# Four transformer layers on one core: capacity search and sorts with buffers of their own, norms on ScalarE, a float32r gate and up product, single PSUM banks, and score steps that give way

## The chip, the cores and the metric

The kernel runs on one core of a Trainium2 chip. The metric is the device time of one execution in microseconds (us). A time is the median of several runs. Besides these there is one execution under the hardware profiler. Its trace gives all durations used here.

The engines of the core are named as the profile names them: PE (TensorE, with PEld for its weight loads), DVE (VectorE), ACT (ScalarE), POOL (GpSimd) and SP (SyncE, which here only issues DMA transfers).

## What is computed

The input is 16 sequences of 256 tokens with 128 features, so 4096 rows. Four layers follow one another. Each adds an attention-like branch and a feed-forward branch to the residual stream, both computed from the same layer norm:

```python
xn = _layernorm(x)
x = x + _L0_attn_ref(xn, ...) + _L0_ffn_ref(xn, ...)
xn = _layernorm(x)
x = x + _L1_attn_ref(xn, ...) + _L1_ffn_ref(xn, ...)
xn = _layernorm(x)
x = x + _L2_attn_ref(xn, ...) + _L2_ffn_ref(xn, ...)
xn = _layernorm(x)
x = x + _L3_attn_ref(xn, ...) + _L3_ffn_ref(xn, ...)
```

- Layer 0: 16-head attention with rotary positions. The feed-forward part has 8 experts of width 512; each token chooses two, and each expert keeps only the `cap` tokens with the highest gates:

```python
cap = max(math.ceil(t * TOP_K * CAP_FACTOR / N_EXPERTS), 1)
for e in range(N_EXPERTS):
    g_masked = jnp.where(has, gate, -jnp.inf)
    vals, idx = jax.lax.top_k(g_masked, cap)
    h = jax.nn.relu(xe @ W1[e]) @ W2[e]
    y = y.at[idx].add(g[:, None] * h)
```

- Layer 1: a linear recurrence along the sequence, a shared expert, and 15 experts of width 128 of which each token takes three.
- Layer 2: attention again, and 8 experts of width 512 of which each token takes one.
- Layer 3: causal attention with a linear position bias per head, an output projection, and a dense gated unit with integer weights:

```python
gate = jnp.einsum('bsd,hd->bsh', x, wg)   # wg = w_gate / 127
up = jnp.einsum('bsd,hd->bsh', x, wu)
h = jax.nn.silu(gate) * up
return jnp.einsum('bsh,dh->bsd', h, wd)
```

## The kernel before

**Tiles.** The rows are cut into 8 blocks of 512 (`BLK`), held in SBUF for the whole kernel (`xb`). A block is two sequences. Expert layers sort their tokens by expert in groups of blocks: two groups of four blocks in layers 0 and 2, four groups of two in layer 1 (`GRP`). Sorted tokens lie in DRAM tables; an expert's tile is 128 rows of such a table.

**Who sets the order.** Nothing is issued while the layers are described. Each engine call goes through `Engine.__getattr__` (L318) into `Plan.add`, which gives it an estimated cost. `Plan.order` (L186) then runs a list schedule over all operations, with a key per operation made of a wanted time per stage (`WANTED`) less the length of the longest chain behind it. It also hands out buffers: a tile has a tag, a tag has a ring of slots, and `room` (L227) says whether a slot is to be had. In the pools `work` and `small` the tiles of a tag are given out in turn, task by task, within one stream (`Plan.run` names the stream). The resulting order is fixed on each engine, and the engines wait for one another through semaphores. Almost every instruction of the profile therefore has one line, L350 (the recorded call); groups are told apart by tile names.

**Attention.** For each sequence `front` (L895) makes the scores once to get row maxima, and `back` (L941) makes them again transposed, with the maxima subtracted, for the exponentials. Head size is 8, so a head's product uses 32 of the 128 rows of the PE array, a strip; heads go two strips at a time. A sequence has 8 score steps in `front` and 8 in `back`; with 16 sequences and three attention layers these are 768 steps. In layers 0 and 2 a `front` step is 4 matmuls of 256 columns and a `back` step 4 of 256 and 2 of 512. In layer 3 each step has 8 strip matmuls and 2 whole-array ones in bfloat16 that hide later keys. When the scheduler takes a step, it looks for another one ready at that moment that uses the other two strips, and weaves the two (`woven`, L74): a pair. Otherwise the step is issued alone.

**PSUM.** There are eight banks. `front` puts its two score tiles into one tile of two banks (`two_banks`, L436), of which there is one in all. One DVE `tensor_reduce` takes the maxima of both banks (in layer 3 two, for the two halves of the queries). The other six banks are single ones (`one_bank`, L439) that everything else shares.

**Norms.** `normalize` (L552) takes mean and variance on DVE (`moments`) and then applies them on DVE, with one `tensor_scalar` for each 128 rows: 4 for each block and layer, 128 in all.

**Capacity search and sorts.** `route_0` (L1090) makes the gates of layer 0 into `g0`. `capacity` (L627) then finds each expert's threshold bit by bit in 30 rounds; a round is a compare and a reduce on DVE, a small matmul `tot_b` that adds over partitions, and three small DVE steps. Its two large tiles `cap_cmp` and `cap_above`, and the tile `m` of `sort` (L1214), share the tag `cap` with three slots; search and sorts run in the same stream, `"sort"`. `ranks` (L673) uses one slot with tag `rank` for both. `sort` gives each token its row in the sorted table; `scatter` (L719) writes the rows there with indirect DMAs on POOL. Only when a group's rows are written can `some_tiles` (L1274) fetch the tiles (`xs`) and run its experts: transpose (`trs`), first product (`ph`), second product (`po`), result back to DRAM. `combine` (L775) gathers results (`yg`) and adds them with the gates, which need the search's result.

**Layer 3's dense unit.** `weights_3` (L1312) loads the integer weights and scales them to float32. `ffn_3` (L1325) runs, for each block and each of three slices of 128 hidden units, two matmuls of 128x512 in float32 (`pp`), a tanh on ACT, two DVE steps, and afterwards the down product.

Of the kernel before, what the change touches and what calls it, by code (L numbers as in the profile page):

```python
# [24 lines left out]
P = 128  # L25
# [8 lines left out]
GRP = {0: 4, 1: 2, 2: 4, 3: 2}  # L34
COLD = 1.2
# [3 lines left out]
    "": (62.9, 0.0, 0.0, 0.0),  # L39
    "att0": (-17.7, 39.8, 36.9, 120.1),  # L40
    "att2": (-125.2, 4.9, -67.1, 45.9),
    "att3": (-85.1, 46.0, 51.1, 102.8),
    "bias2": (-56.2, 153.4, 126.8, 401.9),
    "f3": (166.9, 61.0, 85.4, -51.3),
    "ffn0": (-34.4, 0.0, 32.5, 0.0),
    "ffn1": (2.9, 54.3, 149.0, 145.3),
    "ffn2": (-212.1, 0.0, -158.9, 0.0),
    "kept": (-12.8, 0.0, 0.0, 0.0),
    "rec": (31.1, 105.4, 174.5, 249.2),
    "route0": (-57.1, 0.0, -13.2, 0.0),  # L50
    "route1": (-194.8, -8.3, -27.9, 172.0),
    "route2": (-57.3, 0.0, 43.4, 0.0),
    "sort0": (238.4, 0.0, 310.5, 0.0),
    "sort1": (-45.0, 52.9, 68.6, 170.5),
    "sort2": (-13.5, 0.0, -51.0, 0.0),
    "sum0": (-25.8, 151.2, -71.0, 129.0),
    "sum1": (99.1, 130.3, 136.1, 252.2),
    "sum2": (51.9, 205.8, 84.3, 182.0),
}
EPS = 1e-5  # L60
# [26 lines left out]
class Plan:  # L87
# [98 lines left out]
    def order(self):  # L186
# [40 lines left out]
        def room(o):  # L227

            new = [self.ring_of[x] + (x,) for x in o.tiles if x not in placed]
            for g, turn, task, _, x in new:  # L230
                mine = [y for h, _, _, _, y in new if h is g]
                held = task is not None and (x not in turn[: len(mine)] if task["begun"] else bool(turn))
                if held or len(g["free"]) < len(mine):
                    return g, 0.0, new
            at = [sorted(g["free"])[sum(h is g for h, *_ in new) - 1][0] for g, *_ in new]
            return None, max(at, default=0.0), new
# [18 lines left out]
        while True:  # L255
# [17 lines left out]
            take(o, new, t)  # L273
            cost, pair = o.cost, None
            if o.strips:
                for item in sorted(now[e]):
                    p = item[1]
                    if p.strips and not any(x in o.strips for x in p.strips):
                        short, at, new = room(p)
                        if short is None and at <= t:  # L280
                            now[e].remove(item)
                            heapq.heapify(now[e])
                            take(p, new, t)
                            both = [(x.cost - x.rest, x.rest) for x in (o, p)]
                            cost, pair = max(x for x, _ in both) + max(sum(x for _, x in both) - 0.24 * COLD, 0.0), p
                            break
            if e == "PE" and quartered != bool(o.strips):
                cost, quartered = cost + 0.15 * COLD, bool(o.strips)
# [23 lines left out]
class Engine:  # L312
# [5 lines left out]
    def __getattr__(self, method):  # L318
        real = getattr(self.real, method)

        def call(*args, **kw):
# [8 lines left out]
            if self.name == "PE":  # L330
# [6 lines left out]
                else:  # L337
                    cost = max(size(args[2]), T) / 4800
                    strip = args[1].offset // args[1].ap[0][0]
# [12 lines left out]
        return call  # L352

# [57 lines left out]
def four_layers(ctx: ExitStack, tc: tile.TileContext, a: dict, out: bass.AP, at: dict, found=None):  # L411
# [24 lines left out]
    def two_banks(name):  # L436
        return ps.tile([P, 2, BLK], F32, tag="s", bufs=1, name=name)

    def one_bank(name):  # L439
        return ps.tile([P, BLK], F32, tag="o", bufs=6, name=name)  # L440
# [111 lines left out]
    def normalize(srcs, dst_of, name):  # L552

        mv, rs = moments(srcs, name)
        for i, src in enumerate(srcs):
            dst = dst_of(i)
            for t in range(BT):
                k = i * BT + t
                V.tensor_scalar(
                    dst[:, t, :], src[:, t, :], mv[:, k, 0:1], rs[:, k : k + 1], ALU.subtract, ALU.mult  # L560
                )
# [65 lines left out]
    def capacity(g):  # L627
# [37 lines left out]
        run, _ = ranks(cmp, E0, NT, "cap")  # L665
# [7 lines left out]
    def ranks(m, ne, n, name):  # L673
# [839 lines left out]
```

## Time and profile before

| what | value |
|---|---|
| runs (5): median, lowest, highest | 1570.53, 1549.61, 1579.18 us |
| profiled execution: device time | 1544.55 us |
| its span, first to last instruction | 1542.8 us |
| outside the span | 1.75 us |
| mean granted PE clock | 0.921 |
| DMA moved | 267.35 MB, 173 GB/s over the span |

The page of the profile gives each engine's busy time, then the span in 40 equal slices (38.6 us each) with busy tenths, granted clock and DMA share; then the chain of work that ended last; then the costliest groups of instructions, with their mean duration and the idle time before them. A busy PE in these records is not a PE at its peak: matmuls overlap and a matmul at half clock is busy for longer. Further answers of the trace used here are: windows (busy time of each engine in chosen stretches, with clock and DMA share), one tile's instructions with first and last start, the instructions in order of time, who waited for whom, and groups kept apart by shape.

### The profile page before, as it was taken

To read this page: it belongs to the slowest core of one execution; us is meant where nothing else is said; L and a number is where in the kernel's file an instruction comes from. 1 tells how busy PE (TensorE), PEld (TensorE's weight loads), DVE (VectorE), ACT (ScalarE), POOL (GpSimd) and SP (SyncE) were. 2 spreads that over 40 slices of the span, in tenths; PEclk is the share of its full clock that TensorE was granted. 3 is DMA by queue.
4 is the path that set the end of the run, shared out by engine and by line. 5 is a ranking of instruction groups with operands and counts; after the bars stand their busy time and mean duration, and the time that the engine had idled before them with its cause. 6 is when DMAs were issued, how large, how long until landed. Compare 5 with 4: busy or idle time off the path is not lost. (4 is left out here: it accounts for less than half of the span.)

```text
span 1542.8 us, 35056 instructions
## 1 busy us (share of the span) xinstructions
PE 1380.0 (89%) x12870; PEld 980.0 (64%) x12870; DVE 1026.5 (67%) x2796; ACT 727.3 (47%) x1656; POOL 433.9 (28%) x442
## 2 busy tenths in 40 slices
PE   5568989999998899967998999999999999999997
PEld 4344546777887667755566786466786655566665
DVE  8598985434597799798978536886334746765542
ACT  1104545655543566533666766533554335544324
POOL 1201177400444475667145002351202100100000
PEclk9557979999999999977999999999999979899979
DMA  9702356878876777787666775532684213332210
GB/s 296 230 33 96 117 192 224 269 235 273 280 240 223 213 200 205 199 260 219 196 192 207 245 251 153 188 104 83 214 274 134 97 63 121 99 105 66 92 35 8
DMA packets 229517, 267.35 MB, mean 173 GB/s; under 512 B 19657, under 2 KB 188130, under 8 KB 229346
## 3 DMA queue, kind: packets, MB, share of 16 engines
q1 hardware_dynamic: 217058, 239.92, 49.3%
q0 software_dynamic: 12288, 25.19, 5.3%
q8 instruction: 102, 1.67, 0.4%
q14 instruction: 69, 0.57, 0.1%
HBM read 171.84 MB, written 93.19 MB: 172 GB/s over the span
## 5 line engine op out<-in xcount | busy, mean ns | idle before, releaser
L350 DVE TENSOR_REDUCE mraw<-s 128x4 f32<-128x1024 f32 (+2 forms) x512 | 442.4, 885 | 326.9 <-PE s L350 325.8
L350 ACT ACTIVATE e<-s 128x512 f32<-128x512 f32 (+1 forms) x768 | 378.8, 569 | 225.0 <-PE s L350 220.4
L350 POOL DMA_INDIRECT yg<-result,back_l x192 | 183.9, 958 | 453.6 <-DVE x L350 208.5
L350 PE MATMUL s<-kx,qx 32*128 32x256 f32 (+1 forms) x1536 | 204.2, 344 | 63.8 <-DVE mraw L350 60.6
L710 POOL DMA_INDIRECT rows<-xn,back_l x192 | 192.7, 1004 | 183.8 <-DVE past_l L350 82.3
L350 PEld LDWEIGHTS s<-kx,qx 32*128 32x128 f32 x1536 | 125.5, 197 | 165.3 <-DVE mraw L350 92.3
L350 PE MATMUL av<-e,vaug 128*32 128x256 f32 (+1 forms) x3072 | 204.7, 392 | 0.0
L350 PE MATMUL ph<-xg,we 128*128 128x128 f32 x1296 | 187.3, 288 | 7.2 <-DMA we<-in_experts 4.4
L350 PEld LDWEIGHTS ph<-xg,we 128*128 128x128 f32 x1296 | 164.3, 197 | 37.5 <-issue 15.0
L350 PE MATMUL po<-we,h 128*128 128x128 f32 x1296 | 171.6, 280 | 0.3 <-ACT h L350 0.3
L350 PEld LDWEIGHTS po<-we,h 128*128 128x128 f32 x1296 | 157.5, 194 | 11.1 <-issue 4.8
L350 PE MATMUL s<-qx,kx 32*128 32x256 f32 (+1 forms) x1536 | 155.0, 328 | 6.2 <-DVE half L350 1.9
L350 PEld LDWEIGHTS s<-qx,kx 32*128 32x128 f32 x1536 | 102.0, 196 | 56.1 <-issue 29.3
L350 PEld LDWEIGHTS av<-e,vaug 128*32 128x32 f32 x3072 | 86.7, 115 | 79.7 <-issue 37.9
L350 ACT ACTIVATE h<-ph,we 128x128 f32<-128x128 f32 x336 | 97.5, 372 | 73.3 <-PE ph L350 63.5
L350 PE MATMUL s<-top,shift 32*128 32x512 f32 (+2 forms) x1024 | 128.2, 351 | 0.2
L350 DVE SCALAR_TENSOR_TENSOR x<-yg,gate,x 128x128 f32<-128x128 f32 x192 | 63.9, 343 | 39.0 <-DMA yg<-result,back_l 37.9
L350 PE MATMUL pq<-xT,attn 128*128 128x512 f32 x128 | 83.1, 739 | 2.5 <-DMA attn<-in_attn 2.0
L350 PEld LDWEIGHTS s<-top,shift 32*128 32x128 f32 x1024 | 78.1, 199 | 0.7 <-ACT top L350 0.7
L350 ACT COPY ys<-po 128x256 f32<-128x256 f32 (+2 forms) x104 | 45.8, 450 | 67.2 <-PE po L350 55.4
L350 POOL TENSOR_TENSOR rope<-rope,rope 128x512 f32<-128x512 f32 x16 | 20.4, 1276 | 172.6 <-DVE rope L350 155.2
L350 ACT ACTIVATE h<-ph 128x512 f32<-128x512 f32 x78 | 46.7, 599 | 46.7 <-PE ph L350 46.0
(194 smaller groups left out, 1707.4 us busy)
## 6 DMA issues: line engine op xcount, KB each, us to landing
we<-in_experts SPq DMA_DIRECT2D x78, 512.0 KB
qm<-half SPq DMA_DIRECT2D x48, 512.0 KB
qx<-qm SPq DMA_DIRECT2D x96, 256.0 KB
km<-half SPq DMA_DIRECT2D x48, 512.0 KB
kx<-km SPq DMA_DIRECT2D x96, 256.0 KB
we<-in_experts SPq DMA_DIRECT2D x46, 514.0 KB
we<-in_experts SPq DMA_DIRECT2D x152, 128.5 KB
xs<-rows SPq DMA_DIRECT2D x36, 256.0 KB
```

Of the source, the lines that this page charges most:

```text
L350: self.plan.add(self.name, lambda: real(*args, **kw), [out], ins, cost, sent, strip=strip)
L710: x = nc.gpsimd.indirect_dma_start(out=rows[:, :], out_offset=bass.IndirectOffsetOnAxis(ap=at_, axis=0), in_=src, in_offset=None, bounds_c ...
```

## The change

1. `capacity` has a stream of its own (`"kept"`). Its tiles, now with its own rank tile, keep the tag `cap` with three slots; `sort`'s `m` gets a tag `m` with one slot. `g0` is stored token-major, so that the search reads it through a rearranged view.
2. `normalize` makes one small DVE operation more for each call (minus mean times inverse deviation) and applies the norm with `S.activation(..., AF.Identity, bias, scale)` on ACT.
3. `weights_3` keeps gate and up weights as integers in float32r, and the down weights in float32; the scale 1/127 moves into the tanh's scale and the last addition. `ffn_3` splits the block's normed rows into a float32r part and the rest (one ACT copy, one POOL subtraction, in a slot of the ring `we` that also holds expert weights), and runs two float32r matmuls for each float32 one.
4. All eight banks are single ones. `front`'s two score tiles are two of them, each with its own DVE reduce (in layer 3 two each).
5. In `order`, a score step that finds no partner looks for other work of PE whose key is less than `PATIENCE` (20) above its own and that can go now; if there is some, that goes, and the step waits.
6. The planner's numbers (`WANTED`, `COLD`, a doubled cost for whole-array float32r) are others, and the groups are lists (`GROUPS`) of the same sizes. The attention output tile `y` has one slot in place of two.

```diff
-GRP = {0: 4, 1: 2, 2: 4, 3: 2}
-COLD = 1.2
+GROUPS = {0: (4, 4), 1: (2, 2, 2, 2), 2: (4, 4), 3: (2, 2, 2, 2)}
+COLD = 1.08
...
+PATIENCE = 20.0
...
             if o.strips:
                 for item in sorted(now[e]):
                     p = item[1]
-                    if p.strips and not any(x in o.strips for x in p.strips):
-                        short, at, new = room(p)
+                    if p.strips and not pair and not any(x in o.strips for x in p.strips):
+                        short, at, _ = room(p, new)
                         if short is None and at <= t:
...
+                            pair = item
                             break
+                    elif not p.strips and not instead and item[0][0] - o.key[0] < PATIENCE:
+                        short, at, other = room(p)
+                        if short is None and at <= t:
+                            instead = item + (other,)
+            if pair is None and instead:
+                later(o, t)
+                now[e].remove(instead[:2])
+                heapq.heapify(now[e])
+                _, o, new = instead
...
     def two_banks(name):
-        return ps.tile([P, 2, BLK], F32, tag="s", bufs=1, name=name)
+        return ps.tile([P, 2, BLK], F32, tag="s", bufs=0, name=name)
     def one_bank(name):
-        return ps.tile([P, BLK], F32, tag="o", bufs=6, name=name)
+        return ps.tile([P, BLK], F32, tag="o", bufs=8, name=name)
...
         mv, rs = moments(srcs, name)
+        off = small.tile([P, len(srcs) * BT], F32, tag="off", bufs=2, name=f"off_{name}")
+        V.scalar_tensor_tensor(off, mv[:, :, 0], -1.0, rs, ALU.mult, ALU.mult)
...
-                V.tensor_scalar(
-                    dst[:, t, :], src[:, t, :], mv[:, k, 0:1], rs[:, k : k + 1], ALU.subtract, ALU.mult
-                )
+                S.activation(dst[:, t, :], src[:, t, :], AF.Identity, bias=off[:, k : k + 1], scale=rs[:, k : k + 1])
...
-        run, _ = ranks(cmp, E0, NT, "cap")
+        run, _ = ranks(cmp, E0, NT, "cap", "cap")
...
-                s1 = two_banks(f"s1_{nm}_{m}{u}")
+                s1 = banks(f"s1_{nm}_{m}{u}")
...
-                    V.tensor_reduce(to, s1.rearrange("p j (q k) -> p j q k", q=2), AX.X, ALU.max)
+                for k in range(2):
+                    to = mraw[:, m, 2 * u + k, :]
+                    if causal:
+                        for q, (lo, hi) in enumerate(((0, P), (P, P + T))):
+                            V.tensor_reduce(to[:, q : q + 1], s1[k][:, lo:hi], AX.X, ALU.max)
+                    else:
+                        V.tensor_reduce(to, s1[k].rearrange("p (q k) -> p q k", q=2), AX.X, ALU.max)
...
-        m = work.tile([P, ne, n], F32, tag="cap", bufs=3, name=f"m_{nm}")
+        m = work.tile([P, ne, n], F32, tag="m", bufs=1, name=f"m_{nm}")
...
+        both = work.tile([P, 2, BLK], F32R, tag="we", bufs=4, name=f"x3_{i}")
+        hi, lo = both[:, 0, :], both[:, 1, :]
+        S.copy(hi, xT[3, i])
+        G.tensor_tensor(lo, xT[3, i], hi.bitcast(F32), ALU.subtract)
+        yield
...
-            PE.matmul(pg, w3[0][:, 0, s], xT[3, i], start=True, stop=True)
-            PE.matmul(pu, w3[0][:, 1, s], xT[3, i], start=True, stop=True)
+            for k, to in enumerate((pg, pu)):
+                PE.matmul(to, w3[0][:, k, s], hi, start=True, stop=False)
+                PE.matmul(to, w3[0][:, k, s], lo, start=False, stop=True)
...
-    plan.run(kept(), "sort", "kept")
+    plan.run(kept(), "kept", "kept")
```

## The prediction

> **What bounds the kernel now.** First the page's busy times and slices.
>
> ```profile
> PE 1380.0 (89%) x12870; PEld 980.0 (64%) x12870; DVE 1026.5 (67%) x2796; ACT 727.3 (47%) x1656; POOL 433.9 (28%) x442
> ...
> PE   5568989999998899967998999999999999999997
> ...
> DVE  8598985434597799798978536886334746765542
> ...
> PEclk9557979999999999977999999999999979899979
> ```
>
> PE is busy nearly everywhere, so PE work that goes away shortens the span almost one to one. The exception is the start: for the first six slices (230 us) PE is not full and its clock is low, while DVE is. So I cut the start into windows (busy us, with counts in brackets: PE, PEld, DVE, ACT, POOL; then clock, DMA share, GB/s).
>
> ```profile
> 60.00:100.00 40.00, 25.10 (x80) 15.05 (x80) 32.88 (x88) 3.49 (x7) 6.31 (x5) 0.54 0.32 117
> 100.00:253.00 153.00, 127.47 (x1134) 73.91 (x1134) 128.52 (x269) 68.98 (x136) 57.48 (x54) 0.80 0.37 127
> 253.00:420.00 167.00, 163.98 (x1621) 132.79 (x1617) 69.70 (x114) 95.09 (x196) 52.15 (x52) 1.00 0.82 266
> ```
>
> What begins at 253 us is told by three tiles' own rows (duration min/median/max, first and last start).
>
> ```profile
> L350 PE MATMUL tot_b<-part_b,ones x60: 175/361/384, 69.9 to 156.4; 128*128 128x8 f32 x60
> ```
> ```profile
> L710 POOL DMA_INDIRECT rows<-xn,back_l x64: 971/972/1216, 192.9 to 289.4; - x64
> ```
> ```profile
> L350 PE MATMUL ph<-xg,we x399: 273/275/378, 253.1 to 420.0; 128*128 128x128 f32 x200
> ```
>
> The search runs from 70 to 157 us; the sorts, which share its stream and ring, come after it; the scatters start at 193 and the first expert product at 253. Until then PE has only attention, which goes at the pace of DVE: 161.4 of 193 us busy between 60 and 253. In shorter windows there PE is busy 25.1, 28.0, 35.0, 35.2 and 29.2 us at clocks 0.54, 0.58, 0.97, 0.77 and 0.90, which is 117 us at full clock in 193: a hole of 76 us.
>
> For the rest I read the groups by shape and two waits (total, times, longest).
>
> ```profile
> L350 DVE TENSOR_REDUCE mraw<-s 128x4 f32<-128x1024 f32 x256 | 311.9, 1218 | 183.9 <-PE s L350 183.2
> ...
> L350 ACT ACTIVATE h<-ph,we 128x128 f32<-128x128 f32 x336 | 97.5, 372 | 73.3 <-PE ph L350 63.5 <-issue 4.8 <-PE po L350 3.1
> ...
> L350 DVE TENSOR_REDUCE mraw<-s 128x2 f32<-128x512 f32 x128 | 87.1, 680 | 0.0
> ...
> L350 DVE TENSOR_REDUCE mraw<-s 128x2 f32<-128x256 f32 x128 | 53.9, 421 | 142.9 <-PE s L350 142.6
> ...
> L350 DVE TENSOR_SCALAR xn<-x,mv,ny 128x128 f32<-128x128 f32 x128 | 36.5, 346 | 0.7
> ```
> ```profile
> DVE mraw L350 <- PE s L350: 325.8, 189, 14.7
> ...
> PE s L350 <- DVE mraw L350: 60.6, 83, 3.6
> ```
>
> PE sits idle 60.6 us because the one two-bank tile still has to be read. Last, score steps in layer 3 in order of time: a pair from 1382.46 (8, 8 and 4 matmuls, next step at 1383.69: 1.23 us), and singles at 0.92 to 0.98 us each.
>
> ```profile
> 1382.46 0.45 PE L350 MATMUL s<-qx,kx 32*128 32x256 f32 x8
> 1382.74 0.40 PE L350 MATMUL s<-top,shift 32*128 32x256 f32 x8
> 1383.07 0.61 PE L350 MATMUL s<-laterT,ident 128*128 128x256 bf16 x4
> 1383.69 0.49 PE L350 MATMUL s<-kx,qx 32*128 32x128 f32 x4
> ```
>
> **The change part by part.** All terms are against the profiled execution, 1544.55 us.
>
> *Search and sorts, -40.* In the changed kernel's built order the first group's sort stands on DVE before the first search round, and its scatters on POOL behind 3 operations of attention's rotation (1.28 us each) in place of 17. The 14 that are passed now stand among 64 scatters of 1.0 us, so attention of layer 0 may come later by tens of us, and the experts' work is the cover. On SP, 39 weight loads of 512 KB, which wait for one of four slots, now stand ahead of attention's stores and fetches; that queue already waits 68.2 us for `po` to free slots. The scatters can start near 60 us, and 32 of them with a few rope additions take about 40 us, so experts start near 100 instead of 253. A group has 39 tiles; a tile has 16 matmul instructions at 0.112 us (in runs of 8 the next one starts after 0.89 to 0.90) and a transpose, 1.9 us in all, so 74 us of PE work for a hole of 76, which it also keeps at full clock. DMA is there: share 0.37 before 253 against 0.82 in the expert stage. Bounds: 0 (DVE's pace is the real limit, see rivals) to -75. I take -40, because the window 100 to 253 alone lacks 51 us and the search's 30 rounds still take DVE.
>
> *Float32r, -20.* `pp` before: 4 instructions in 1.72 to 1.91 us, 1.81 as a rule, 24 times, 43 us. After, 4 float32r matmuls of 512 columns. No row has one over the whole array. Upper bound: as long as a float32 instruction, 0.45, nothing gained. Lower: two strips' float32r matmuls of 512 columns took 0.24 until the next instruction; 4 x 0.24 = 0.96, gain 24 x 0.85 = 20. I take that, the same format and width. The 8 ACT copies (0.59 us) and 8 POOL subtractions (1.28 us) are hidden: POOL is busy 11 us of the last 343; without cover, 15 us. The split rows take one of the four expert weight slots for a block's length; `ph` waits for weights 4.4 us today, and I leave that at nothing.
>
> *Pairs, -19.* By the built orders, 155 pairs after and 122 before, of 768 steps; 458 single steps against 524. Layer 3: 45 to 53 pairs, each saving 2 x 0.95 - 1.23 = 0.67: 5. Layers 0 and 2: back with back 33 to 43; a single back step takes 0.48 to 0.56, a pair 0.68, so 0.4 each: 4. Front with front 0 to 51; a single takes 0.43, the pair isn't in the trace, between 0.43 (like 8 back matmuls of 256 columns, 0.34, and the way out) and 0.86; I take 0.48, saving 0.38: 19, or 0 at the bad end. Front with back 43 to 7, each losing 0.28: -10. Sum 18 to 19; bounds 0 and -30.
>
> *Single banks, -25.* A `front` step can go while the one before is being read. Of the 60.6 us of idle PE, the part where DVE itself is behind remains. Bounds 0 and -61; I take 25, less than half, because DVE gets slower (next term). With scores able to hold all eight banks, whatever needs one queues behind them on PE.
>
> *DVE, +10.* Reduces: 256 x (2 x 0.680 - 1.218) = 36; causal 128 x (2 x 0.421 - 0.680) = 21; and 128 x (2 x 0.29 - 0.421) = 20, where 0.29 for 128 columns continues the step from 680 to 421. Norms: -36.5, and 32 small ones at 0.16, +5. Net +46 on 1026, which is hidden wherever PE ends last; bounds 0 and +46. From 420 to 860 us DVE is busy 371 of 440, so some shows: +10, like the shallow end.
>
> *Norms on ACT, 0.* 128 more on an engine that is 47% busy. The nearest row is the `h` activation above, 372 ns with one per-partition operand; on 128x512 a second one (`v`, 777 ns, against `h1s`, 692) adds 85. So 0.37 to 0.46 each, 48 to 58 us of ACT; a block's chain grows by up to 4 x (0.457 - 0.346) = 0.4 us, 11 us over 24 later blocks if nothing else ran (exponentials queue behind it). Bounds -5 and +11.
>
> The Trainium skill, "ScalarE: Activation LUTs", section "What ACT_TABLE_LOAD costs", speaks against this move: 186 ns plus 0.833 ns per element plus about 93 ns for each pointer operand, so an estimate of 479 ns where DVE took 346. The row of 372 ns agrees with the 387 that it gives for one operand. By the page's figure the uncovered chain would grow by 13 us in place of 11.
>
> Sum: 1544.55 - 40 - 20 - 19 - 25 + 10 = 1450 us, 6% less. The median before, 1570.53, is 1.7% over the profiled time; at the same ratio the median after is 1475.
>
> **The rivals.** Times are medians, profiled sum x 1.017.
>
> *DVE becomes the bound; slower.* Place: 420 to 860 us, where DVE is at 84% and gets longer reduces in the same queue as the inverse roots, routes and combines. Where PE waits for DVE today it looks like 660 to 720 us: PE busy 41.6 of 60 at a mean clock of 0.72, half of its full work. Each us of span that turns into this costs about 0.5. To undo 95 us, 190 us of span must turn; to end over 2% slower (31 us more), about 250. At 290 it is (1450 + 145) x 1.017 = 1622. Against it: DVE's total would be 1073 of 1450, 74%.
>
> *The hole fills, but nothing comes of it.* If DVE, not PE, paces everything up to 860 us, earlier experts only move PE's idle time. Then the first term is 0 and the fourth 10: 1505 x 1.017 = 1531. For it: DVE is at 84% both from 60 to 253 and from 420 to 860. Against: from 253 to 420 PE is 98% busy at full clock while DVE is at 42%.
>
> *Better than the sum.* The hole closes (-75) and the reads' wait goes (-50): 1390 x 1.017 = 1414.
>
> *It doesn't do what it says.* The give-way rule leaves 458 steps alone; if woven front steps gain nothing and float32r runs at float32's rate, the sum is 1450 + 20 + 19 = 1489, median 1514.
>
> **How the numbers follow.** My sum (1440 to 1500) 0.42; better 0.16; hole without gain or no gain in the matmuls, together 0.24, about all under the 2% line at 1539; a mixture within 2% 0.09; slower 0.09. Two per cent is about what a measurement of this kernel tells from no change. So faster 0.82, same 0.09, slower 0.09. The range leaves out half of the better case and everything slower than 1550: 1410 to 1550.
>
> **What would show it.** First `ph` near 100 us instead of 253 and a clock near 1 from 100 on (first term); `pp` runs of 4 in about 1 us (second); `s` waiting for `mraw` well under 60 us (fourth); DVE at 1070 us, ACT near 780. Wrong if `ph` starts early and PE's busy time between 253 and 860 falls with the span no shorter, or if waits of PE for DVE grow.

## The result and the profile after

The changed kernel takes 1564.97 us (median of 45 runs, 1551.35 to 1583.85), the kernel before 1562.7 us (87 runs, 1537.04 to 1592.87). The ratio is 1.0074, 95% interval 1.0056 to 1.0092: no change by the 2% line, a little slower if anything. (The ratio is taken over executions in the faster of two states that the same program shows, so it isn't the quotient of the two medians.) The forecast of 1475 and its range of 1410 to 1550 both miss.

Most signs that the prediction named came nonetheless; a clock near 1 from 100 us on did not (0.89 from 100 to 253 us, below), and DVE is busy 1048 us, not 1070. These are rows of three tiles of the changed kernel (first and last start behind the colon):

```profile
L374 PE MATMUL tot_b<-part_b,ones x60: 172/350/382, 64.1 to 199.9; 128*128 128x8 f32 x60
...
L751 POOL DMA_INDIRECT rows<-xn,back_l x192: 968/972/1540, 48.9 to 1209.7; - x192
...
L374 PE MATMUL ph<-xg,we x1296: 272/275/583, 112.9 to 1289.7; 128*128 128x128 f32 x186
```

Scatters start at 49 us in place of 193, experts at 113 in place of 253; the search itself ends 44 us later. The groups by shape and the waits of PE (total, times, longest):

```profile
L374 DVE TENSOR_REDUCE mraw<-s 128x2 f32<-128x512 f32 x512 | 316.1, 681 | 106.6 <-PE s L374 105.9
...
L374 DVE TENSOR_REDUCE mraw<-s 128x1 f32<-128x256 f32 x256 | 93.7, 416 | 54.1 <-PE s L374 53.0
...
L374 DVE TENSOR_REDUCE mraw<-s 128x1 f32<-128x128 f32 x256 | 57.6, 279 | 0.0
...
L374 ACT ACTIVATE xn<-x,off,ny 128x128 f32<-128x128 f32 x128 | 52.6, 488 | 32.1 <-DVE off L374 32.1
...
L374 PE MATMUL pp<-x,w 128*128 128x512 f32 x96 | 33.4, 478 | 0.0
```
```profile
PE tot_b L374 <- DVE part_b L374: 39.5, 19, 6.7
PE s L374 <- DVE mraw L374: 21.1, 38, 2.9
PE trx L374 <- ACT xn L374: 18.5, 4, 11.9
```

The same tiles in the kernel before:

```profile
L350 PE MATMUL pp<-xT,w 128*128 128x512 f32 x96 | 45.1, 596 | 0.0
```
```profile
PE trx L350 <- DVE xn L350: 24.0, 7, 11.3
...
PE tot_b L350 <- DVE part_b L350: 18.5, 18, 4.9
```

`pp` is busy 33.4 us; before it was 45.1. The wait for `mraw` fell from 60.6 to 21.1 us. Yet the page shows more busy PE, not less:

```profile
PE 1410.1 (90%) x12870; PEld 1009.9 (65%) x12870; DVE 1048.1 (67%) x3213; ACT 776.3 (50%) x1792; POOL 441.2 (28%) x450
...
PE   5466999999999989999899998999999998999998
...
PEclk9559899999999987999899995979998997998989
```

The same 12870 matmuls take 30 us more of busy time, and the last row tells why: 12 of its slices have a digit under 9, and the same row of the kernel before has nine such slices. So I split the PE time of both profiles in three with the records of the clock: work (busy time, counted half where the clock was half, for the clock knows only these two values), loss (the other half of that time) and idle.

| us | work at full clock | lost at half clock | idle | span |
|---|---|---|---|---|
| before | 1280.1 | 99.9 | 162.8 | 1542.8 |
| after | 1266.0 | 144.1 | 153.8 | 1563.9 |
| difference | -14 | +44 | -9 | +21 |

By stage, in windows (the columns are those of the prediction's windows), first the changed kernel, then the three late stretches of the kernel before:

```profile
100.00:253.00 153.00, 138.20 (x1166) 102.28 (x1166) 101.56 (x214) 66.28 (x135) 47.74 (x47) 0.89 0.59 188
253.00:420.00 167.00, 154.99 (x1342) 110.67 (x1345) 117.42 (x329) 80.32 (x165) 60.73 (x59) 0.96 0.61 190
420.00:860.00 440.00, 411.83 (x3644) 301.59 (x3636) 314.34 (x947) 263.61 (x630) 159.17 (x164) 0.91 0.67 207
860.00:1200.00 340.00, 318.15 (x2980) 225.21 (x2980) 235.24 (x795) 161.64 (x377) 94.81 (x96) 0.87 0.47 146
1200.00:1564.00 364.00, 341.82 (x3579) 237.49 (x3578) 204.03 (x579) 182.14 (x437) 33.57 (x33) 0.90 0.36 114
```
```profile
420.00:860.00 440.00, 393.17 (x3398) 294.25 (x3397) 371.04 (x1183) 234.23 (x532) 228.96 (x232) 0.95 0.71 215
860.00:1200.00 340.00, 319.27 (x3228) 233.91 (x3228) 193.72 (x505) 180.95 (x476) 67.62 (x69) 0.97 0.57 179
1200.00:1543.00 343.00, 318.25 (x3300) 205.38 (x3298) 188.69 (x397) 136.98 (x298) 11.39 (x11) 0.92 0.24 77
```

Between 860 and 1200 us PE is as busy as before (318 and 319 us), but its clock is 0.87 in place of 0.97, and it gets 248 fewer matmuls done. Added up from the start, work at full clock stands as follows: at 253 us 143 before and 158 after; at 420 us 307 and 306; at 860 us 681 and 681. So the early experts bring 15 us, and these are gone 167 us later. The 15 us are clock, not idle time: ahead of 253 us PE lost 42 us at half clock before and 25 after, and was idle for 68 and 70. Behind 860 us the changed kernel has less work left (585 against 599 us) and takes 21 us longer for it.

The executions without a trace say the same, for each reports its span and mean clock. Over 33 executions of the kernel before the span falls by 12.3 us for each 0.01 of clock (correlation -0.95), over 47 of the changed kernel by 14.2 (-0.91): one and the same program moves by nearly 50 us (1541 to 1589) as its clock goes from 0.920 to 0.880. The correlation alone doesn't say what drives what, but 0.01 of clock over 1560 us is 15.6 us of PE time at full clock, so the slope is about what lost clock costs. The medians are 1563.6 us at 0.903 and 1563.2 at 0.890. Taken to a clock of 0.903, the changed kernel would stand at 1563.2 - 1.3 x 14.2 = 1545: by this estimate the change is worth up to 19 us of PE work and waits (7, if the ratio of 1.0074 is taken in place of the medians), and loses them to the clock. (The profiled execution of before, with 0.921 and 1542.8 us, was about the best of all, so the table's +21 is more than the medians' difference.)

### The profile page after: what moved, and what is told of

The parts are those of the page before. It is cut to its first block, busy times and chain, and to the rows that moved or that the text cites. A ratio compares the mean times of both kernels' runs of the same rounds, so it can differ in the third digit from the quotient of the medians.

```text
span 1563.9 us, 35816 instructions
## 1 busy us (share of the span) xinstructions
PE 1410.1 (90%) x12870; PEld 1009.9 (65%) x12870; DVE 1048.1 (67%) x3213; ACT 776.3 (50%) x1792; POOL 441.2 (28%) x450
## 3 DMA queue, kind: packets, MB, share of 16 engines
q8 instruction: 103, 1.69, 0.4%
## 4 chain that ended last, share of the span: by engine, by line
PE 47%; DVE 9%; issue 2%; ACT 2%; DMA 1%; POOL 0%; ACTq 0%; POOLq 0%; SPq 0%
PE s L374 19%; PE av L374 7%; PE po L374 7%; PE ph L374 5%; DVE mraw L374 4%; PE pp L374 2%; PE pq L374 2%; DMA yg<-result,back_l 1%; PE trs L374 1%; DVE x L374 1%; PE tra L374 1%; PE pv L374 1%; PE lg L374 1%; PE trm L374 1%; PE trx L374 1%
## 5 line engine op out<-in xcount | busy, mean ns | idle before, releaser
L374 DVE TENSOR_REDUCE mraw<-s 128x2 f32<-128x512 f32 (+2 forms) x1024 | 460.2, 514 | 160.7 <-PE s L374 158.9
L374 PE MATMUL s<-kx,qx 32*128 32x256 f32 (+1 forms) x1536 | 175.2, 348 | 28.7 <-DVE mraw L374 18.4
L374 PE MATMUL ph<-xg,we 128*128 128x128 f32 x1296 | 194.1, 296 | 6.5 <-DMA we<-in_experts 4.2
L374 PEld LDWEIGHTS ph<-xg,we 128*128 128x128 f32 x1296 | 170.7, 204 | 38.7 <-issue 16.8
L374 PE MATMUL po<-we,h 128*128 128x128 f32 x1296 | 178.1, 286 | 0.9 <-ACT xg L374 0.7
L374 PEld LDWEIGHTS s<-kx,qx 32*128 32x128 f32 x1536 | 108.6, 196 | 104.0 <-issue 43.0
L374 PE MATMUL s<-qx,kx 32*128 32x256 f32 (+1 forms) x1536 | 159.9, 342 | 5.3 <-DVE mraw L374 2.7
L374 ACT ACTIVATE h<-ph,we 128x128 f32<-128x128 f32 x336 | 97.4, 372 | 63.7 <-PE ph L374 60.6
L374 DVE SCALAR_TENSOR_TENSOR x<-yg,gate,x 128x128 f32<-128x128 f32 x192 | 72.7, 387 | 39.9 <-DMA yg<-result,back_l 38.7
L374 PE MATMUL pq<-xT,attn 128*128 128x512 f32 x128 | 83.9, 746 | 2.9 <-DVE mraw L374 1.8
L374 ACT COPY ys<-po 128x256 f32<-128x256 f32 (+1 forms) x104 | 46.6, 449 | 74.8 <-PE po L374 69.4
L374 ACT ACTIVATE xn<-x,off,ny 128x128 f32<-128x128 f32 x128 | 52.6, 488 | 32.1 <-DVE off L374 32.1
```

Source lines behind the costliest of these rows:

```text
L374: self.plan.add(self.name, lambda: real(*args, **kw), [out], ins, cost, sent, strip=strip)
```

## The experiments

Times are medians; a ratio is to runs of the kernel before on the same chip, taken as above, with its 95% interval. Work, lost and idle in the tables are us of the one profiled execution, so they need not add up to the median.

**What the clock follows.** In the changed kernel a stretch of half clock lies between 941 and 982 us. Windows, then PE's rows in order of time (start, us):

```profile
940.00:960.00 20.00, 16.98 (x86) 10.83 (x87) 13.92 (x47) 0.69 (x1) 6.93 (x8) 0.53 0.59 172
960.00:980.00 20.00, 18.00 (x113) 13.96 (x112) 12.94 (x73) 4.78 (x12) 6.59 (x7) 0.50 0.34 92
```
```profile
944.12 0.79 PE L374 MATMUL s<-kx,qx 32*128 32x128 f32 x4
944.72 0.62 PE L374 MATMUL s<-shift,slopes 32*128 32x128 f32 x4
945.28 0.61 PE L374 MATMUL s<-later,ident 128*128 128x256 bf16 x2
945.81 0.79 PE L374 MATMUL s<-kx,qx 32*128 32x128 f32 x4
```

PE is busy 85 to 90% of it, with lone score steps of layer 3, most of whose matmuls use two strips of 32 rows: 1.69 us a step, where a single step took 0.92 at full clock. So I wrote a kernel of such matmuls alone, without gaps (`clock_alone`); `strips(k)` issues one float32r matmul of 512 columns on each of k strips, `mixed(a, b)` a matmuls on one strip and then b over the whole array:

```diff
+        strips(4, 150)
+        strips(2, 150)
+        strips(4, 80)
+        strips(1, 150)
+        strips(2, 150)
+        strips(3, 150)
...
+        mixed(full[0], 7, 1, 20)
...
+        mixed(full[3], 2, 1, 50)
```

> No part of the reference is computed (the output is left over from the matmuls); stages of float32r matmuls of 512 columns run without a gap, each followed by a dense stage of four strips of 32 rows side by side. Activity theory (the clock follows the share of the array's rows in use: after a window of 3.4 us below about 0.36 of the array it falls to half, above 0.40 it rises): one strip (0.25) falls to half within two windows though PE never waits; two strips out of the dense stage (0.50) stay at full clock; two strips straight behind one strip (0.50 of half a clock = 0.25) stay at half; three strips behind those (0.75 of half = 0.38) undecided, three strips out of the dense stage full; 7 one-strip matmuls to 1 of 128 rows (0.34) half, 4:1 (0.40) undecided, 3:1 (0.44) and 2:1 (0.50) full. Busy theory (the clock follows idle gaps alone): clock 1.0 in every stage after the first 4 us. Chance theory (the clock falls for reasons outside of the kernel): falls that do not keep to the stages.

The page, then windows in the stages two strips, one, two behind one, three behind two, three behind four, 7:1, 4:1, 3:1, 2:1, and the whole array behind one strip (busy PE and PEld, DVE and POOL, clock, DMA share, GB/s):

```profile
PE 796.8 (97%) x5340; PEld 568.7 (69%) x5340; DVE 5.8 (1%) x9; POOL 0.2 (0%) x4
...
PE   4999999999999999999999999999999999999994
...
PEclk9999955555599999655595555955568555595598
```
```profile
50.00:80.00 30.00, 30.00 (x269) 26.60 (x266) 0.00 (x0) 0.00 (x0) 1.00 0.01 1
105.00:158.00 53.00, 53.00 (x126) 40.89 (x125) 0.00 (x0) 0.00 (x0) 0.50 0.00 0
160.00:222.00 62.00, 62.00 (x294) 47.84 (x292) 0.00 (x0) 0.00 (x0) 0.50 0.00 1
230.00:258.00 28.00, 28.00 (x375) 24.47 (x374) 0.00 (x0) 0.00 (x0) 1.00 0.01 2
280.00:310.00 30.00, 30.00 (x402) 26.40 (x399) 0.00 (x0) 0.00 (x0) 1.00 0.01 2
340.00:406.00 66.00, 66.00 (x134) 39.69 (x132) 0.00 (x0) 0.00 (x0) 0.50 0.00 0
436.00:505.00 69.00, 69.00 (x127) 36.23 (x126) 0.00 (x0) 0.00 (x0) 0.50 0.00 0
535.00:602.00 67.00, 67.00 (x117) 32.41 (x117) 0.00 (x0) 0.00 (x0) 0.50 0.00 0
630.00:712.00 82.00, 82.00 (x133) 34.35 (x132) 0.00 (x0) 0.00 (x0) 0.50 0.00 0
...
780.00:808.00 28.00, 28.00 (x125) 23.07 (x123) 0.00 (x0) 0.00 (x0) 1.00 0.00 0
```

PE never waits, and the clock goes by stage. One whole-array matmul took 227 ns at full clock, and so did one on a single strip; that gives the share of the array in use. One strip (0.25) falls within 5 us of its start. Two strips at 112 ns a matmul (0.51) keep the full clock when they come out of a dense stage, but the same two strips behind one strip go at 213 ns (0.27) and stay at half for all their 64 us: at half clock they do too little to get it back. Three strips (142 ns at half clock, 0.40) get it back within a window. 3:1 and 2:1 fell against expectation; each change between a strip and the whole array takes time (a round of 3:1 took 1.32 us and one of 2:1 1.09, where matmuls of 227 ns make 0.91 and 0.68: 0.41 us for the two changes of a round), so their matmuls took 316 and 346 ns on average at full clock and the shares were 0.31 and 0.33, not 0.44 and 0.50. (The expectation's unit was 6% larger: its 0.36 and 0.40 are 0.38 and 0.43 here.) The busy theory and the chance theory are out.

The clock of both large kernels changes only at multiples of 3.41 us. For each such window I worked out the share in the same unit (float32 matmuls, which take twice as long, counted double). Where the clock was full and the share under 0.38, it fell in 17 windows of 17 before and 30 of 30 after; from 0.38 to 0.46 in 2 of 14 and 3 of 13; above 0.46 in 2 of 328 and 0 of 295. A low share can come from thin matmuls or from waits. Half-clock time grew by 97 us in all (244 to 342). Falls behind a window in which PE was over 80% busy led to 14 us of it before and 55 after, the others to 229 and 287; with the line at 75% it is 17 and 130, the others 225 and 211, mostly because one stretch of 61 us near the start stands behind a window that was 79% busy. So at least 41 of the 97 us come out of windows in which PE seemed full; how much of the rest began with a wait isn't settled. The stretch from 941 us did: PE was 65% busy in the window ahead of it (share 0.33), and the lone steps behind it kept the clock down.

The Trainium skill, "TensorE: Matmul & The Clock Gate", Part 1, ties the gate to how busy PE is and asks that no gap exceed about 3.4 us. The window agrees with the 3.41 us here. The rest doesn't: `clock_alone` is at half clock through hundreds of us without a gap.

**The order kept, the array filled.** `after_6banks` is the changed kernel with six shared banks, `after_6banks_fill` the same order with a matmul more on an idle strip, into banks that nothing reads, for each two strip matmuls of a lone step (1941 more in all).

```diff
-        return ps.tile([P, BLK], F32, tag="o", bufs=8, name=name)
+        return ps.tile([P, BLK], F32, tag="o", bufs=6, name=name)
...
+                if m is None and k < o.steps and k % 2:
+                    self.fill(o.used[k])
```

> Control for the next run: the changed kernel with six PSUM banks in the shared ring instead of eight, and nothing else changed (the planner makes its order for six). Clock theory: the span of the changed kernel (1563.9 us) is lost to half clock, not to a want of banks, so this is within 1540 to 1600 us, with 300 us or more at half clock. Bank theory (what is gained by single banks is what eight of them allow): 1600 us or more.

> Same order as after_6banks. For each pair of strip matmuls of a score step that goes alone, one more strip matmul on an idle third strip is issued into a spare bank that nobody reads, so such a step works on three strips instead of two, and takes no longer if strips run beside each other. Clock theory (the clock falls to half after a 3.4 us stretch in which columns times used rows are below about 0.36 of a full array, and lone two-strip steps are below that): time at half clock falls to under half of after_6banks's, mean clock above 0.95, and the time falls by 50 to 100 us against after_6banks. Waits theory (PE's idle time and the other engines set the end, the low clock only follows from it): the same half-clock time within 15 per cent, and no gain or up to 30 us more, from 970 added matmuls.

1769.23 us without and 1687.94 us with the added matmuls (ratio of the latter to before 1.0871, 1.0711 to 1.1032). The four executions without them took 1725.41 to 1777.88 us, the profiled one being the longest; the four with them took 1676.74 to 1696.91, the profiled one being the shortest. The pages:

```profile
PE 1589.2 (89%) x12870; PEld 1111.8 (63%) x12870; DVE 1051.8 (59%) x3213; ACT 785.9 (44%) x1792; POOL 441.4 (25%) x450
...
PEclk9568999799999899769998968785669997768788
```
```profile
PE 1498.1 (89%) x14811; PEld 1065.9 (64%) x14811; DVE 1049.1 (63%) x3213; ACT 786.1 (47%) x1792; POOL 442.8 (26%) x450
...
PEclk9567999799799789978999997889999997898899
```

1941 matmuls more, and in these two PE is busy 91 us less: half-clock time fell from 581 to 319 us. The shortest execution without the added matmuls had a clock of 0.872, so 441 us of half clock (span times twice the missing share); those with them had 0.895 to 0.906, 316 to 356 us. Work that serves nothing bought 81 us by the medians and 49 between the shortest executions. That thin steps, and not the order alone, made a good part of this loss is shown here, for the order of six banks. The mean clock stayed under the 0.95 that was hoped for, and half-clock time didn't fall to under half.

The control itself went against the clock theory, which had it at 1540 to 1600 us; above 1600 was the bank theory's place. Two banks fewer undo most of the pairing: the planner's order has 67 pairs and 634 lone steps, with eight banks 155 and 458.

**Parts undone.** First the give-way rule and the planner's numbers:

```diff
-            if pair is None and instead:
+            if False:
```
```diff
-COLD = 1.08
+COLD = 1.2
...
 WANTED = {
...
-    "sort0": (44.1, 0.0, 85.1, 0.0),
+    "sort0": (238.4, 0.0, 310.5, 0.0),
```

> The changed kernel without the give-way rule: a score step without a partner is issued at once, as before the change; the planner makes its order anew. If the rule is what puts lone steps into runs at half clock: half-clock time falls from 342 us to 250 or less and the time by 20 to 50 us (1515 to 1545). If the single banks or the planner's numbers do it: within 15 us of the changed kernel, half-clock time 300 us or more.

> The changed kernel with the planner's numbers of before (WANTED and COLD; the new stage w3 keeps its value). If the new numbers are what spoils the change: 1450 to 1510 us. Clock theory with the rule or the banks as its cause: 1540 to 1620 us and 300 us or more at half clock, as the numbers were not made for this version.

1637.71 us (1.0505, 1.0362 to 1.0648) and 1600.82 us (1.0303, 1.0173 to 1.0432). Undoing either makes the kernel slower still, so neither spoils the change by itself; the first lies outside both of its expected ranges, the second in the clock theory's. `after_old_numbers` has more pairs than any kernel (183) and is slower than the changed kernel, so pairs alone don't tell the time. Then search (which also gives `y` its two slots back), banks, and float32r (item 3 of the change taken back; its edit isn't shown):

```diff
-        m = work.tile([P, ne, n], F32, tag="m", bufs=1, name=f"m_{nm}")
+        m = work.tile([P, ne, n], F32, tag="cap", bufs=3, name=f"m_{nm}")
...
-            plan.run(kept(), "kept", "kept")
+            plan.run(kept(), "sort", "kept")
```
```diff
-                s1 = banks(f"s1_{nm}_{m}{u}")
+                s1 = two_banks(f"s1_{nm}_{m}{u}")
```

> The changed kernel with the capacity search back on its old shared buffers and in its old stream (the due times stay the new ones). Clock theory (the early experts only move dense matmuls out of the stages behind 253 us, where the lone score steps then lose the clock): no slower than the changed kernel, 1540 to 1575; half-clock time behind 253 us under 220 us against about 270. The prediction's sum: the search's 40 us come back on top, 1590 to 1620, experts from about 250. Disorder theory (any edit that reshuffles the order, without due times made for it, costs 20 to 70 us whatever it does): 1585 to 1635 with more half-clock time and no term that explains it.

> The changed kernel with the front's two-bank tile and the joint reduces of before (six single banks and one pair). The prediction's sum: the wait of score steps for mraw returns from 21 to about 60 us, DVE loses 36 us of work, time 1580 to 1595. Clock theory: the time follows half-clock time, +1 us for each 2 us of it, whatever the wait does. Disorder theory: 1585 to 1635.

> The changed kernel with layer 3's gated matmuls in float32 as before. The prediction's sum: layer 3's busy time returns from 33 to 45 us and the others with it, +20 us, 1580 to 1590. Clock theory: the slower passes keep the array as full as it can be for twice as long, so part of it is given back in clock, 1565 to 1580, with less half-clock time than the changed kernel's 342. Disorder theory: 1585 to 1635.

| | time, ratio to before | work | lost | idle |
|---|---|---|---|---|
| `after_no_search` | 1669.34, 1.0749 (1.0664 to 1.0834) | 1282 | 190 | 196 |
| `after_two_banks` | 1577.20, 1.0182 (1.0086 to 1.0278) | 1271 | 114 | 164 |
| `after_no_f32r` | 1615.30, 1.0420 (1.0330 to 1.0511) | 1303 | 160 | 148 |

With the joint banks the wait of `s` for `mraw` returns from 21.1 to 61.3 us and the time rises by about 1%, under the prediction's 25 us and no more than an order alone can make, as the next runs show. (Its profile is of its shortest execution, 1551.93 us.) The other two cost far more than their terms (105 and 50 us for 40 and 20), and most of the search's is loss and idle time, not work. The clock theory had expected no loss at all without the early search, and under 220 us of half clock behind 253 us; there are 331, so that fell.

**The same instructions in another order, and parts alone.** To see what an order for which the due times were not made costs, one planning factor was moved by 0.01; that changes no instruction. Float32r and the give-way rule were put into the kernel before, each alone.

```diff
-COLD = 1.2
+COLD = 1.19
```
```diff
-COLD = 1.08
+COLD = 1.07
```

> The kernel before with its planner's factor COLD at 1.19 in place of 1.20: the same instructions and due times, another order (562 lone score steps and 103 pairs against 524 and 122). By the prediction's price of a pair (0.58 us) 19 pairs fewer cost 11 us: 1570 to 1580. Disorder theory (an order for which the due times were not made costs 20 to 70 us): 1585 to 1635, and the loss shows as half-clock time and idle time without any instruction changed. Neither: within 5 us of the kernel before, then the undone parts of the changed kernel measured what they seem to.

> The changed kernel with COLD at 1.07 in place of 1.08 (480 lone steps and 144 pairs against 458 and 155). Price of pairs: +6 us, 1570. Disorder theory: 1585 to 1635. If it is no slower than 1570, the undone search (+104), give-way rule (+73) and float32r (+50) are worth about that in this order.

> The kernel before with layer 3's gated matmuls in float32r alone (552 lone steps and 108 pairs). The prediction's sum: -20 us, 1535 to 1545. By what its undoing cost (50 us): 1505 to 1515. Disorder theory: the 20 us and the loss of the order together, 1560 to 1610; its half-clock time is then over the 244 us of before.

> The kernel before with the rule alone that a score step without a partner gives way to other work (484 lone steps and 142 pairs). The prediction's price of a pair: 20 more, -12 us, 1545 to 1555. By what its undoing cost (73 us): 1480 to 1500. Clock theory: the rule parts dense work from lone steps or mixes them, so the time follows the half-clock time, 1 us for 2. Disorder theory: 1575 to 1625.

| | time, ratio to before | work | lost | idle |
|---|---|---|---|---|
| `before_cold119` | 1577.74, 1.0151 (1.0025 to 1.0278) | 1280 | 138 | 158 |
| `after_cold107` | 1605.22, 1.0307 (1.0213 to 1.0402) | 1275 | 132 | 200 |
| `before_f32r` | 1687.00, 1.0825 (1.0689 to 1.0960) | 1267 | 199 | 214 |
| `before_give` | 1666.80, 1.0715 (1.0612 to 1.0818) | 1267 | 191 | 198 |

Two rows of `before_f32r`, the clock of its page and `pp`:

```profile
PEclk9556878999999988779999875899958996779986
```
```profile
L354 PE MATMUL pp<-x,w 128*128 128x512 f32 x96 | 29.1, 436 | 0.0
```

The part does what it says (`pp` 45.1 to 29.1 us, work 13 us less), and the kernel is 8% slower, since the order that comes out loses the clock and waits. A factor of 0.01 costs 1.5 and about 2.3% (1.0307 against 1.0074). The first could still be the price of its lost pairs (1570 to 1580 foreseen), the second can't (1570). The two parts alone lie above all of their ranges, the disorder theory's too. So neither a part undone nor a part alone measures the part: the eleven orders so far lie within 1259 and 1303 us of work (the six-bank ones, with 1335 and 1371, aside; why the first of them has 69 us more work than the changed kernel with the same matmuls isn't known), while loss and idle time together run from 263 to 413 us.

**Due times fitted anew.** For both kernels, and for the changed one without its search, the due times were fitted by random search over the planner's own model, with its planned end plus a modelled half-clock loss as the aim; the kernel before got the factor 1.08 as well. Nothing else differs:

```diff
-COLD = 1.2
+COLD = 1.08
...
 WANTED = {
...
```

> The changed kernel, due times alone fitted anew with the clock's rule in the aim: planned end 1525 us with 74 us of modelled half-clock loss, against 1546 and 103 with the change's own due times. Disorder theory (the time is set by how well the due times fit the order): spans were 2 to 18 us over the planned end in four of the six profiles of its family, so 1530 to 1550, faster than both kernels, half-clock time under 300 us. The prediction's sum in place of that: the change has given what it can, 1555 to 1575.

> The kernel before, with the changed kernel's planning factor (1.08) and due times fitted anew in the same way: planned end 1541 us, 63 us of modelled half-clock loss. Theory that the change is worth little once both fit: within 15 us of after_retuned, 1540 to 1560. The prediction's sum: 75 us or more over after_retuned, 1600 to 1625. Clock theory: more score steps stand alone than in after_retuned (568 against 482) but fewer in runs with nothing between, so its half-clock time is no longer.

> The changed kernel without the search's part, due times fitted anew in the same way: planned end 1619, 95 us of modelled loss. If the 104 us that the search's undoing cost came from due times that did not fit: 1550 to 1590. If the other parts need the early search: 1610 to 1650.

> A second fit of the changed kernel, planned end 1522, modelled loss 83. Two fits of one kernel within 15 us of one another; if they are further apart, the planned end doesn't tell the chip's order of them.

> A second fit of the kernel before (planned end 1540 us, modelled half-clock loss 70). Worth-little theory: within 15 us of the three fits of the changed kernel, 1540 to 1560. Prediction's sum, a part of it at least: 25 us or more above them all, 1575 or more.

> A third fit of the changed kernel (planned end 1533, modelled loss 71). Worth-little theory: 1535 to 1560, the groups overlap. Prediction's sum, a part of it at least: this one and the two other fits all 25 us or more under before_retuned2.

| | time | ratio to before | work | lost | idle |
|---|---|---|---|---|---|
| `before_retuned` | 1541.50 | 0.9877 (0.9562 to 1.0192) | 1283 | 124 | 129 |
| `before_retuned2` | 1785.96 | 0.9950 (0.9900 to 0.9999) | 1290 | 176 | 317 |
| `after_retuned` | 1554.16 | 0.9938 (0.9885 to 0.9992) | 1276 | 117 | 145 |
| `after_retuned2` | 1539.70 | 0.9873 (0.9704 to 1.0042) | 1275 | 125 | 141 |
| `after_retuned3` | 1763.88 | 0.9880 (0.9843 to 0.9917) | 1274 | 183 | 312 |
| `after_no_search_retuned` | 1637.36 | 1.0497 (1.0334 to 1.0660) | 1265 | 185 | 195 |

The chip of `before_retuned2` and `after_retuned3` ran the kernel before in 1782.74 us, too; why that one is slower isn't known (idle PE is 317 us against 129 in `before_retuned`), and only ratios of it are used. The fits of the kernel before lie at 0.988 and 0.995, those of the changed kernel at 0.994, 0.987 and 0.988. The groups overlap; the two that were timed side by side on the slower chip differ by 0.7%, and two fits of one kernel by 0.6 to 0.7%. So about 1% is left of the change with due times fitted to both (1.6% between the far ends of the slower chip's two intervals), where the prediction had 6%. Of the expectations the worth-little theory's held (on the slower chip by the ratios); the disorder theory's 1550 us for `after_retuned` was missed by 4. Windows of `before_retuned` and of `after_retuned`:

```profile
860.00:1200.00 340.00, 334.99 (x3496) 245.35 (x3494) 216.47 (x531) 196.15 (x496) 59.20 (x61) 1.00 0.58 186
```
```profile
860.00:1200.00 340.00, 317.34 (x3112) 224.60 (x3111) 248.32 (x832) 169.86 (x399) 105.38 (x107) 0.90 0.52 161
```

Here again the kernel with late experts keeps the clock and the other one doesn't. But over the whole span the two lose the same, 124 and 117 us: up to 253 us it is 54 and 27, behind 860 us 31 and 57. So with due times fitted to each, the clock no longer parts them; the changed kernel has 7 to 8 us less work and 12 to 16 us more idle time. Without the search's part the other parts are 5% slower than the kernel before even with a new fit. So in the orders that this planner makes they need it; why, these runs don't tell.

The best that the changed kernel reaches with due times fitted anew is 1.2 to 1.3% under the kernel before; by the 2% line that is no change, and the kernel before reaches 1.2% with a fit of its own.

## Why the prediction was wrong

The step that failed first is its opening one: "PE work that goes away shortens the span almost one to one", with the cover that the early experts fill a hole "which it also keeps at full clock". It took the clock at which PE's work runs as given. The profile of before showed the flaw, for its fourth and sixth slices have PE at 8 tenths and the clock at 0.7, but the prediction put low clocks down to waits. That is not all: of the 115 us between the sum's -94 and the +21 of the traces, 44 are clock, 25 are PE work and 46 idle time that were to go and didn't. By its terms:

- *Search, -40.* Mechanism right: `ph` at 113 us, and the work done by 253 us grew by 15. But the stage behind had no hole to leave: before, 253 to 420 us was 164 of 167 us busy at full clock with the very tiles that now come early. After it, that stage does 148 us of work. By 420 us nothing is left of the gain. Nor did the early work fill idle time at the start (68 us before, 70 after). The rival "the hole fills, but nothing comes of it" saw this outcome and gave the wrong reason: DVE sets no such pace, as its busy time between 420 and 860 us fell from 371 to 314.
- *Float32r, -20.* Right: `pp` at full clock is 43.5 us before and 25.5 after, -18.
- *Pairs, -19.* Wrong in size and sign. 155 pairs came, but all matmuls of `s` and `av` took 594 us at full clock after and 589 before. The guess of 0.38 us saved for two front steps, marked as not in the trace, carried the term; its bad end, nothing, was nearer.
- *Single banks, -25.* The wait for `mraw` fell by 39.5 us, and others came: the search's `tot_b` now waits 39.5 us for `part_b` against 18.5. PE's waits for DVE fell by 43.5 us in all (127.4 to 83.9), those for ACT, which makes `xn` now, rose by 31.8 (17.3 to 49.1). Total idle time fell by 9 us for this term, the search's and DVE's together, where the sum had 55.
- *DVE, +10; norms on ACT, 0.* DVE grew by 22 us, not 46: split reduces are 681 ns long, but the next one starts earlier, so 512 of them are busy 316 us, not 349. No wait for it shows. `xn` on ACT took 488 ns, above the upper end of 457; the estimate of 479 from the Trainium skill's "ScalarE: Activation LUTs", section "What ACT_TABLE_LOAD costs", was nearer. The wait of `trx` for `xn` didn't grow (24.0 to 18.5 us).
- *What the sum lacked.* Clock, +44. The sum gave -94 against the profiled execution, the traces have -18 + 5 - 1 (other work) - 9 + 44 = +21. By the medians of all executions, and by the estimate above, the clock took back the 7 to 19 us that were left of the gain.

"Wrong if `ph` starts early and PE's busy time between 253 and 860 falls with the span no shorter" was the sign that it named, and it came half: the span is no shorter, but the busy time rose there by 10 us, at a lower clock.

What is shown: 44 of the missing 115 us are half-clock time; the clock follows the share of the array in use; thin steps in a row can lose it and don't regain it; the order sets how much, and with due times fitted to both kernels about 1% is left. What is not shown is why this order lost more than the one before. That the early experts leave the late score steps without dense work agrees with four profiles (behind 860 us 38 us lost before and 75 after, and 31 and 57 in the fits; of 1312 `ph` matmuls 372 lie behind 860 us before and 300 after). It doesn't agree with four others in which the experts come late, `ph` from 247 to 302 us on: `before_give`, `before_f32r` and the two without the search's part lose 74 to 100 us there. No run moved the experts alone, and the cause stays open.

## What to carry to other kernels

Read busy time together with the granted clock: split an engine's span into work at full clock, loss and idle time before pricing a change, and ask of each stage what fills the array. A hole ahead of a full stage is worth little if the work that fills it is taken out of that stage, as here by 420 us. Where a planner sets the order, measure what a change of no consequence costs first (here 1.5 to 2.3%), and compare versions only with due times fitted to each.

## What was not expected of the hardware

- With no gap in PE's records, the clock stayed at half for 55 us of one-strip matmuls and the 64 us of two-strip ones behind them; the same two strips ran at full clock out of a dense stage. The state depends on what came before.
- 1941 matmuls into banks that nobody reads made a kernel 81 us faster by the medians, 49 between the shortest executions.
- A float32r matmul of 512 columns over the whole array takes 227 ns at full clock, as long as one on a single strip, and four strips side by side take 227 ns together as a rule.
- A round of matmuls on one strip and then over the whole array took 0.41 us longer than its matmuls alone, for the two changes.
- The same program on the same data moves between 1541 and 1589 us, and 12.3 us of that go with each 0.01 of mean clock.
